# Order of the first DMA requests in a gated-FFN and state-space kernel: two tiles of token block 1 ahead of the first LoRA factors

## The chip, the cores and the metric

The kernel runs on one core of one Trainium2 chip. The metric is the device time of the kernel in microseconds (us). Three runs of the kernel before the change gave 439.82, 440.07 and 442.02 us; their median is 440.07 us.

## The reference

```python
x = L0_attn_u                                   # (2, 1024, 512) float32
xn = _layernorm(x, axis=-1)                     # over the 512 features of a token
s = _L0_attn_ref(xn, ...)                       # S4: a causal convolution of length 512 along the
                                                # features, plus D * xn; its kernel K comes from
                                                # a 64-state system by way of an FFT
g = _silu(_L0_ffn_ref(xn, w1, w3, w2, A1, B1, A3, B3, A2, B2))
x = x + s * g
...
def _lora_linear(x, w, a, b):                   # w, with a LoRA pair a (16 x in), b (out x 16)
    base = jnp.einsum('bsd,od->bso', x, w)
    low = jnp.einsum('bsr,or->bso', jnp.einsum('bsd,rd->bsr', x, a), b)
    return base + low * 2.0
h1 = _lora_linear(x, w1, lora_A1, lora_B1)      # 512 -> 1376
h3 = _lora_linear(x, w3, lora_A3, lora_B3)      # 512 -> 1376
return _lora_linear(silu(h1) * h3, w2, lora_A2, lora_B2)
```

All of it is computed in float32.

## The kernel before

**Tiling.** The 2048 tokens are four blocks of 512 (blocks 0 to 3), each of four tiles of 128 tokens by 512 features (256 KB). The 1376 hidden features are five pairs of 128-wide chunks and a last chunk of 96. The LoRA pairs are not applied to the tokens: TensorE multiplies the small factors (L410), and the product is added to the weights in SBUF, so that one weight matrix is left. The large products are made by a Strassen-like scheme (sums of token blocks and sums of weight blocks, seven products in place of eight, twice nested), whose sums run on VectorE.

**Order of the work.** TensorE, VectorE, ScalarE and GpSimd have a schedule written out by hand: the program's order is the order on each engine, and every engine takes its own instructions strictly in order. The main part is put into a heap of events with places (the function `at`), and run off in order of place. DMAs are issued from two queues, those of SP (`nc.sync`) and ScalarE (`nc.scalar`). ScalarE issues DMAs from the same stream as its compute, so a DMA issue that waits holds up what stands behind it on ScalarE.

**Semaphores of the DMAs.** In the built program the DMAs of both queues take eight semaphores in turn, in program order. A DMA that takes a semaphore for the second time waits at its issue until the DMA that had it before has landed. The first eight DMAs wait for nothing. The ninth waits for the first, the tenth for the second, and so on.

**The start (L1020 to L1074).** These steps are what the change and the prediction touch:

- `load_x(0)` at L1020 (the DMA itself is L236): four tiles of block 0, SP takes tiles 0 and 2, ScalarE takes tiles 1 and 3.
- `load_lora` at L1027: the first factors. The inner factors a1 and a3 (16 x 512, 32 KB each, L399, tile `lo_d`) and the columns 768 to 1375 of the outer factors b1T and b3T (16 x 608, 38 KB each, L400, tile `lo_h`). SP loads a1 and b1T into partitions 0 to 15, ScalarE loads a3 and b3T into partitions 32 to 47.
- The activation at L1028 loads ScalarE's table ahead of its use.
- `load_x(1)` at L1029: four tiles of block 1, all on SP.
- `load_last` (L502): the last chunk of w1T and w3T. `load_pair(0)` (L429): the first weight pair. Blocks 2 and 3 (L236, tile `t_in`), the second pair and two more sets of factors follow on SP.
- `keep_warm` (L1046): 18 dummy products, 36 matmul instructions, that keep TensorE busy until the data comes.
- `lora_last` (L410, banks y) and `pair_products(0, 0)` (L410, banks x and w): the first real products of TensorE. They need the first factors.
- `take_last` (L520): ScalarE takes the two y banks out to SBUF, scaled.
- `norm_stats` (L252, L253), `norm_root` (L286, L57 to L66, L289) and `normalize` (L298 on ScalarE for tiles 0 and 2, L302 on GpSimd for tiles 1 and 3): the layer norm of block 0. VectorE makes the statistics.
- `merge_last` (L528) on GpSimd adds the taken-out products to the last chunk of weights.
- `transpose` (L309): TensorE turns the four tiles of block 0, and ScalarE copies them out (L317). The products of the last chunk follow (L799).
- The same layer norm is made for block 1 (L252 to L289, L298, L302), whose tiles are turned at L329.

On ScalarE the order is therefore: DMA issues, table load, the two L520, the two L298 of block 0, the copies L317. On TensorE it is: L1046, L410, L309, L799.

## Time and profile before

| what | value |
|---|---|
| median of three runs | 440.07 us |
| profiled execution, its own time | 439.75 us |
| its span, first to last instruction | 437.7 us |
| granted TensorE clock, mean | 0.999 |
| busy TensorE / VectorE / GpSimd / ScalarE | 431.7 / 314.3 / 211.4 / 146.8 us |
| moved by DMA in the span | 53.60 MB, mean 122 GB/s |

The profile is of one execution. "Busy" is the time in which an engine had an instruction in work. A row of a timeline gives the start, the duration, the engine, the line, the operation, the tile that is written and those that are read, the count and, in brackets, the idle time ahead of it and what ended it. SPq and ACTq are the issuing of DMAs by SP and ScalarE, PEld is the loading of weights into TensorE.

### The profile page before, as it was taken

The numbers are of one execution on the slowest core, as the hardware profiler recorded it, in microseconds if no ns is written. First come the engines' busy times: TensorE is split into PE (matmuls) and PEld (weight loads), VectorE is DVE, ScalarE is ACT, GpSimd is POOL, SyncE is SP. The second block draws the span as 40 slices with busy tenths as digits, with TensorE's granted clock in tenths as the row PEclk, the third lists the DMA queues.
The fourth block names the chain that finished last, engine by engine and source line by source line (L and its number), as shares of the span: only waits on it lengthen the run. The fifth ranks groups of instructions, "written<-read, shape, count | busy, mean of one in ns | idle before, by whom it ended". The sixth has DMA issues, their size and how long they took to land.

```text
span 437.7 us, 5081 instructions
## 1 busy us (share of the span) xinstructions
PE 431.7 (99%) x1664; PEld 267.7 (61%) x1664; DVE 314.3 (72%) x531; ACT 146.8 (34%) x301; POOL 211.4 (48%) x159
## 2 busy tenths in 40 slices
PE   7999999999999999999999999999999999999996
PEld 7645334344444444444443447888898999989896
DVE  5989997975873687368736786979786885653234
ACT  2897233344344334433443242211101212112221
POOL 1628185799599558945894378400000122222221
PEclk9999999999999999999999999999999999999999
DMA  8931312016105200430054536395901833422211
GB/s 242 368 96 27 130 59 91 0 50 206 35 24 158 84 25 24 148 113 24 25 173 164 168 98 209 114 355 195 361 3 74 303 124 96 145 96 97 77 68 48
DMA packets 35465, 53.60 MB, mean 122 GB/s; under 512 B 4688, under 2 KB 21520, under 8 KB 35312
## 3 DMA queue, kind: packets, MB, share of 16 engines
q1 hardware_dynamic: 31824, 49.55, 33.9%
q10 hardware_dynamic: 3616, 3.74, 2.9%
q8 instruction: 13, 0.21, 0.2%
q14 instruction: 12, 0.10, 0.1%
HBM read 33.88 MB, written 19.40 MB: 122 GB/s over the span
## 4 chain that ended last, share of the span: by engine, by line
PE 88%; DVE 8%; ACT 1%; issue 1%; DMA 1%; POOL 0%; SPq 0%; DVEq 0%; ACTq 0%; POOLq 0%
PE x L799 44%; PE y L799 22%; PE w L799 12%; PE aux L979 2%; PE w L979 2%; PE aux L994 2%; DVE xt L355 2%; DMA s<-in_x_dram 1%; DVE s L485 1%; PE y L410 1%; DVE w L473 1%; PE y L572 1%; PE aux L754 1%; ACT c L259 1%; DVE aux L1379 1%
## 5 line engine op out<-in xcount | busy, mean ns | idle before, releaser
L1382 POOL TENSOR_TENSOR o<-o,xin 128x512 f32<-128x512 f32 (+1 forms) x17 | 23.3, 1369 | 132.5 <-DMA g<-g_dram 68.6
L885 POOL TENSOR_TENSOR s<-c,s 128x512 f32<-128x512 f32 (+1 forms) x44 | 66.0, 1505 | 11.5 <-ACT c L877 7.7
L819 ACT COPY s<-x 128x512 f32<-128x512 f32 (+1 forms) x54 | 31.6, 585 | 82.7 <-PE x L799 77.7
L799 PE MATMUL x<-t_in,s 128*128 128x512 f32 (+1 forms) x148 | 55.4, 500 | 0.0
L823 DVE TENSOR_TENSOR s<-s,y 128x512 f32<-128x512 f32 (+1 forms) x54 | 36.4, 681 | 18.4 <-PE y L799 10.6
L919 POOL TENSOR_TENSOR s<-ua_three,s 128x512 f32<-128x512 f32 x20 | 30.2, 1510 | 21.6 <-DVE s L823 21.6
L799 PEld LDWEIGHTS x<-t_in,s 128*128 128x128 f32 x148 | 26.8, 190 | 22.4 <-issue 12.4
L919 POOL TENSOR_TENSOR ua_three<-ua_three,s 128x512 f32<-128x512 f32 x20 | 31.2, 1560 | 14.0 <-DVE s L823 14.0
L799 PE MATMUL y<-t_in,s 128*128 128x256 f32 (+1 forms) x108 | 35.8, 458 | 0.0
L1404 ACT COPY z<-x 128x256 f32<-128x256 f32 x24 | 8.8, 371 | 70.4 <-PE x L799 70.3
L1379 DVE TENSOR_TENSOR aux<-aux,m 128x384 f32<-128x384 f32 x32 | 18.1, 566 | 15.7 <-PE aux L979 14.1
L919 POOL TENSOR_TENSOR s<-u_three,s 128x512 f32<-128x512 f32 x20 | 28.4, 1423 | 1.8 <-ACT c L877 1.0
L877 ACT ACTIVATE c<-c 128x512 f32<-128x512 f32 x40 | 25.2, 632 | 10.4 <-DVE c L919 10.2
L799 PEld LDWEIGHTS y<-t_in,s 128*128 128x128 f32 x108 | 20.2, 190 | 11.1 <-issue 9.1
L919 POOL TENSOR_TENSOR u_three<-ua_three,u_three 128x512 f32<-128x512 f32 x10 | 15.9, 1589 | 20.5 <-DVE u_three L823 18.2
L842 ACT COPY w<-x 128x512 f32<-128x512 f32 (+1 forms) x37 | 21.1, 571 | 11.8 <-PE x L799 11.7
L799 PE MATMUL x<-t_in,w 128*128 128x512 f32 x40 | 21.0, 606 | 0.0
L799 PE MATMUL x<-xr,w 128*128 128x512 f32 x40 | 20.8, 613 | 0.0
L799 PE MATMUL x<-xt,w 128*128 128x512 f32 x40 | 20.6, 597 | 0.0
L799 PE MATMUL x<-xr,s 128*128 128x512 f32 x40 | 20.5, 614 | 0.0
L799 PE MATMUL x<-xt,s 128*128 128x512 f32 x40 | 20.4, 592 | 0.0
L799 PE MATMUL y<-xt,w 128*128 128x512 f32 x40 | 19.9, 592 | 0.0
(321 smaller groups left out, 911.7 us busy)
## 6 DMA issues: line engine op xcount, KB each, us to landing
g_dram<-s SPq DMA_DIRECT2D x40, 256.0 KB, 2.2
g<-g_dram SPq DMA_DIRECT2D x10, 512.0 KB, 5.8
xin<-in_x_dram SPq DMA_DIRECT2D x16, 256.0 KB, 2.7
out_dram<-o SPq DMA_DIRECT2D x14, 256.0 KB, 2.0
t_in<-g_dram SPq DMA_DIRECT2D x6, 512.0 KB, 4.2
t_in<-in_x_dram SPq DMA_DIRECT2D x8, 256.0 KB, 5.4
w_a<-in_w2T_dram SPq DMA_DIRECT2D x2, 1024.0 KB, 7.1
room<-g_dram SPq DMA_DIRECT2D x4, 512.0 KB, 6.1
```

Source lines behind the costliest of these rows:

```text
L355: nc.vector.tensor_tensor(t[name - 1], one, other, add if name == 2 else sub)
L799: nc.tensor.matmul(ps[:, cols], lhsT=lhsT, rhs=rhs if parts == 1 else rhs[:, cols], start=first and i == 0 and part == 0, stop=i == len(pa ...
L819: nc.scalar.copy(t, self.x)
L823: nc.vector.tensor_tensor(t, t, self.y, add)
L842: nc.scalar.copy(self.w, self.x)
L877: nc.scalar.activation(c, c if src is None else src, AF.Silu)
L885: nc.gpsimd.tensor_tensor(g, act, g, mult)
L919: (nc.vector if o < 20 else nc.gpsimd).tensor_tensor(to, a, b, add)
L979: nc.tensor.matmul(to[:, n * P : (n + 1) * P], lhsT=x_, rhs=by, start=start, stop=True, skip_group_check=True,)
L1379: nc.vector.tensor_tensor(y[:, P:], y[:, P:], m[:, n * P : (n + 3) * P], add)
L1382: (nc.vector if last else nc.gpsimd).tensor_tensor(o, o, self.xin[h][:, cols], add)
L1404: nc.scalar.copy(t, xb)
```

## The change

The first eight DMAs in program order are now the four tiles of block 0, tiles 0 and 1 of block 1, a1 and a3. Then come b1T and b3T, and then tiles 2 and 3 of block 1. Tiles 1 and 3 of block 1 go to ScalarE's queue in place of SP's. ScalarE's table load stands behind all of these. No DMA and no compute instruction is added or taken away, and the order of the compute instructions on each engine stays as it was.

```diff
-    def load_x(b):
+    def load_x(b, some=range(NTT)):
...
-        for tt in range(NTT):
+        for tt in some:
...
-            queue = nc.scalar if b == 0 and tt % 2 else nc.sync
+            queue = nc.scalar if b < 2 and tt % 2 else nc.sync
...
         if d is not None:
             queue.dma_start(out=lora["d"][rows, :], in_=d)
+        if h is None:
+            return
         queue.dma_start(out=lora["h"][rows, : hi - lo], in_=h[:, lo:hi])
...
     factors = (a1, b1T), (a3, b3T)
-    for v, f in enumerate(factors):
-        load_lora((nc.sync, nc.scalar)[v], v, *f, LSPLIT, HID)
+    x_in[1] = load_x(1, (0, 1))
+    for v, (d, h) in enumerate(factors):
+        load_lora((nc.sync, nc.scalar)[v], v, d, None, LSPLIT, HID)
+    for v, (d, h) in enumerate(factors):
+        load_lora((nc.sync, nc.scalar)[v], v, None, h, LSPLIT, HID)
+    x_in[1] += load_x(1, (2, 3))
     nc.scalar.activation(warm, warm, AF.Silu)
-    x_in[1] = load_x(1)
     make_upper_triangular(nc, tri, 1.0, diag=True)
```

## Prediction

> **What bounds the kernel now.** I read the page's engine rows first, then the list of what TensorE (PE) waited for, then the timelines of the first 12 us engine by engine, then the DMA views of that stretch.

> ```profile
> PE 431.7 (99%) x1664; PEld 267.7 (61%) x1664; DVE 314.3 (72%) x531; ACT 146.8 (34%) x301; POOL 211.4 (48%) x159
> ...
> PE w L1046 <- POOL ident masks.py:199: 1.4, 1, 1.4
> PE aux L309 <- ACT s L298: 1.0, 1, 1.0
> ```

> The second and third lines are the whole of PE's waits in 437.7 us. PE waits 1.4 us at the start for the identity, 1.0 us for the first normalized tile of block 0, and from 11.0 us on it waits for nothing that the list shows: its instructions follow one another to 434.1 us. The end is therefore the start of the first transpose (L309, at 10.99 us) plus a fixed 426.7 us. Whatever moves L309 moves the end one for one; what is moved elsewhere is free until it makes PE wait. A little can be absorbed: between 53 and 59 us three matmuls start 0.1 to 0.2 us late, 0.4 us in all, since VectorE (DVE) has only just made their operands.

> So the question is what sets 10.99 us. The timelines of PE, ScalarE (ACT) and DVE from 5 to 12 us (start, duration):

> ```profile
> 5.58 2.50 PE L1046 MATMUL w<-ident 128*128 128x128 f32 x17
> 8.01 1.13 PE L410 MATMUL y<-lo_h,lo_d 16*128 16x96 f32 x16
> ...
> 9.66 0.37 PE L410 MATMUL w<-lo_h,lo_d 16*128 16x256 f32 x1
> 10.99 0.44 PE L309 MATMUL aux<-ident,s 128*128 128x128 f32 x2 [0.96 <-ACT s L298]
> ```
> ```profile
> 9.17 0.87 ACT L520 ACTIVATE c<-y 128x384 f32<-128x384 f32 x2 [5.09 <-PE y L410]
> 10.12 1.52 ACT L298 ACTIVATE s<-s,shift,rs_y 128x512 f32<-128x512 f32 x2
> ```
> ```profile
> 6.40 0.69 DVE L252 BATCH_NORM_STATS2 stats<-s 128x6 f32<-128x512 f32 x1 [0.84 <-DMA s<-in_x_dram]
> 7.13 0.18 DVE L253 BATCH_NORM_AGGREGATE mv<-stats 128x2 f32<-128x6 f32 x1
> ...
> 9.93 0.16 DVE L289 SCALAR_TENSOR_TENSOR shift<-mv,rs_y 128x4 f32<-128x4 f32 x1
> ```

> L309 needs L298, and L298 has two conditions of almost the same age. One is DVE's shift, ready at 9.93 + 0.16 = 10.09 us; the chain of waits goes this way, back to tile 2 of block 0, which landed at 6.38. The other is ACT's own order: the two L520 end at 9.17 + 0.87 = 10.04 us. They wait for PE's L410, which starts at 8.01, and L410 waits for the four factors. Their landings:

> ```profile
> lo_h<-in_b1T_dram SPq DMA_DIRECT2D x1, 38.0 KB, 5.6
> lo_h<-in_b3T_dram ACTq DMA_DIRECT2D x1, 38.0 KB, 5.8
> ```

> Issued at 2.09 and 2.11 us, they land at 7.7 and 7.9. The dummy products would let PE go at 7.92 (the last starts at 7.80, and they start 0.11 apart). The factors therefore come just in time, with no reserve, and ACT's branch trails DVE's by 0.05 us.

> **The change part by part.**

> *Block 0 lands earlier.* Tiles 2 and 3 landed at 6.38 and 6.96 (issued at 1.15, 5.2 and 5.8 us to landing) while the factors were coming in. With tiles 0 and 1 of block 1 behind them in place of the factors, I expect them between 4.9 and 5.3: 1.05 MB at the 370 GB/s of the first row below end at 4.8. DVE then loses its 0.84 us of waiting: the shift is ready at about 9.2. Alone this is worth at most 0.08 us, since the L520 hold ACT until 10.04 even with the factors as early as now. That is the bound on the gain.

> *The factors land later.* 512 KB now go ahead of them. The DMA traffic in three stretches (last two columns: busy share, GB/s):

> ```profile
> 2.00:5.00 3.00, 3.00 (x16) 3.00 (x16) 1.10 (x3) 1.49 (x2) 0.00 (x0) 1.00 1.03 370
> 5.00:7.00 2.00, 2.00 (x13) 2.00 (x13) 1.13 (x3) 0.00 (x0) 0.00 (x0) 1.00 1.04 131
> 7.00:10.00 3.00, 3.00 (x34) 2.46 (x32) 2.59 (x14) 0.83 (x2) 0.00 (x0) 1.00 1.04 343
> ```

> While the factors are under way (5 to 7 us) the engines are as busy as before but move a third; afterwards the rate returns. So the tiles ahead pass at the full rate: 524 kB / 370 GB/s = 1.4 us, and the slow stretch follows, as long as now. The last factor lands at 7.9 + 1.4 = 9.3 us. Two checks on this: b1T and b3T are the ninth and tenth DMA now, so they wait for tiles 0 and 1 of block 0, landed at 3.84 and 4.02, and are issued at 3.9 and 4.0 in place of 2.1, still 2 us before their turn; and the first other tiles of block 1 are issued at about 5.1, behind them, and share the slow stretch as block 1's tile 0 did before (issued at 3.86). Lower bound: no slow stretch at all; 1.57 MB + 0.14 MB at 370 GB/s end at 6.6, landing about 7.0, so PE is not held and the change gives -0.1. Upper bound: the 524 kB pass at 131 GB/s, 4.0 us, so +3.9. I take 1.4, since the rows on both sides of the slow stretch carry tiles of just this kind at 343 and 370.

> *What the late factors hold.* L410 moves from 8.01 to about 9.4, the L520 from 9.17 to 10.57, ACT is free at 11.44 in place of 10.04, L298 starts at 11.45 in place of 10.12, and L309 at 12.3 in place of 10.99: +1.3 us. PE's own order alone (L410 issued until 9.87 + 1.4 = 11.3) would not bind. Behind ACT's L520 also wait the copies L317, behind PE's L410 everything; GpSimd's (POOL) L528 need the L520 too and move with them. DVE's merges (L420 at 15.99, after a wait for PE of 0.2) move with PE. I let 0.2 us be absorbed, half of the late starts found at 53 to 59 us: **+1.1 us**.

> *Block 1's statistics.* DVE reaches them at 9.2 in place of 10.0, and needs tiles 0 to 3 at 9.2, 10.0, 10.8 and 11.6. They land by about 6.5 (0, 1) and 9.6 to 10.4 (2, 3; the total of bytes up to there is unchanged, and tile 3 landed at 10.36). No wait. This branch was not late before: L298 of block 1 ended at 16.59, PE came to L329 at 16.82. Worth nothing.

> *Later loads on SP.* The same eight semaphores, two requests fewer on SP. The first weight pair now waits for the landings of a1, a3, b1T and b3T (about 8.6 to 9.3) and was issued from 8.37 to 9.94 before: no change over 0.3 us. Its pieces landed at 12.5 to 14.7, and DVE takes them from 16.0: 1.3 us of cover, more if PE is late.

> *ACT's table load.* It ran from 2.58 to 3.86. It now stands behind tile 3 of block 1, whose issue waits for tile 3 of block 0 (at the latest 6.96, as now): issue to 7.4, load to 8.7, the small activation to 8.9. The first L520 came at 9.17: hidden by 0.3 us in that worst case, by 1.5 us or more with the later factors.

> [...] The factors go to partitions 0 to 15 and 32 to 47, and the row says 131 GB/s for 2 us. [...] The row shows 2 us, and 3 from the end of block 0's data (4.8) to the last landing (7.9); I follow it.

> **Rivals.**

> *Hidden (439.6 to 440.3).* The slow stretch comes from factors and tiles of both queues in each other's way, and is shorter when the factors come in one after another, or the 512 KB fill time that was lost. The factors land by 8.4, the time changes by -0.1 to +0.4. For it: four factor loads with 48 KB each, issued from 29.3 to 30.6 us with nothing beside them, landed in 1.9 to 2.0 us. Against it: at 5 to 7 us the tiles beside them were slow as well, and tiles are beside them again.

> *The clock falls (443.3).* PE has a hole of 1.4 us at 8 to 9.4 in which it had none, then 1.9 us of 16-row matmuls, then a second hole of 1.0 us. If TensorE's granted clock drops over this, the transposes start at the pace of the beginning: dummy products start 0.213 us apart until 6.4 us, 0.112 after, and that stretch, 5.1 us, cost 23 x 0.101 = 2.3 us. With +1.3 and less absorbed, +3.5. It decides from a hole that the clock does not forgive. Against it: the hole of 1.1 us before L309 cost no clock; the L309 start 0.109 apart.

> [...]

> *The slow stretch grows (442 to 443.6).* The tiles ahead of the factors also come in at the slow rate: up to the upper bound of +3.9.

> *It gains.* Only if L309 moved forward by 2.2 us; the L520 forbid this.

> **How the numbers follow.** 0.5% is 2.2 us, about what a measurement of this kernel can tell from no change. The sum against the profiled execution: 439.75 (span 437.7 and 2.05 around it) + 1.1 = 440.85. The median of the runs lies 0.3 above that execution, which would give 441.2; I say 441.0. Chances: forecast (+0.4 to +2.2) 0.65; hidden 0.19; clock 0.08; slow stretch beyond 2.2 us 0.06; a gain 0.02. Faster 0.02, within 0.65 + 0.19 = 0.84, slower 0.14. The range goes from 439.6 (hidden, -0.1) to 442.9, into the slow cases, and leaves the clock's case and the far end out.

> **What would show it.** Right: DVE's wait before L252 gone and the shift near 9.2; landings of b1T and b3T near 9.3; a wait of PE before L410; L298 of block 0 right behind the L520 at about 11.4; L309 near 12.3; no other PE wait. Wrong: factors landed by 8.0 (hidden), L309 starts 0.21 apart (clock), ACT's L520 behind the table load, or a new wait of DVE for block 1.

## The result and the profile after

The changed kernel takes 443.05 us (median of nine runs, 441.54 to 444.96) against 440.07 us before. The ratio is 1.0063, with a 95% interval of 1.0041 to 1.0085: slower by 0.6%. The profiled execution is the slowest of the nine, 444.96 us, with a span of 442.9 us and a mean granted clock of 0.991.

The engine row and the row of the clock in 40 slices, from the page of the changed kernel, and then the whole list of what TensorE (PE) waited for. Lines of the file have moved: L412 was L410, L522 was L520, L801 was L799, L1051 was L1046.

```profile
PE 434.5 (98%) x1664; PEld 269.6 (61%) x1664; DVE 314.8 (71%) x531; ACT 147.0 (33%) x301; POOL 211.6 (48%) x159
...
PEclk9699999999999999999999999999999999999999
```
```profile
PE y L412 <- DMA lo_h<-in_b1T_dram: 2.6, 1, 2.6
PE w L1051 <- POOL ident masks.py:199: 1.4, 1, 1.4
PE y L801 <- DVE w_a L422: 0.4, 1, 0.4
PE aux L309 <- ACT s L298: 0.4, 1, 0.4
```

The same row of the clock from the page of the kernel before:

```profile
PEclk9999999999999999999999999999999999999999
```

Two things are new. PE waits 2.6 us for the factors, where it waited for none. And the second slice of the clock row has a 6 where every slice had a 9: for a stretch behind the start, TensorE got half its clock (0.50, in the table of stretches below). The landings of b1T and b3T, issued at 4.03 and 4.22 us, come to 9.9 and 10.1:

```profile
lo_h<-in_b1T_dram SPq DMA_DIRECT2D x1, 38.0 KB, 5.9
lo_h<-in_b3T_dram ACTq DMA_DIRECT2D x1, 38.0 KB, 5.9
```

The timelines of PE and ScalarE (ACT), start and duration, show the chain that the prediction followed:

```profile
9.96 1.20 PE L412 MATMUL y<-lo_h,lo_d 16*128 16x96 f32 x15 [2.58 <-DMA lo_h<-in_b1T_dram]
...
12.75 1.97 PE L309 MATMUL aux<-ident,s 128*128 128x128 f32 x8 [0.38 <-ACT s L298]
14.51 1.91 PE L309 MATMUL y<-ident,s 128*128 128x128 f32 x8
...
19.25 1.13 PE L412 MATMUL aux<-lo_h,lo_d 16*128 16x256 f32 x8
```
```profile
11.12 0.87 ACT L522 ACTIVATE c<-y 128x384 f32<-128x384 f32 x2 [3.79 <-PE y L412]
11.88 1.51 ACT L298 ACTIVATE s<-s,shift,rs_y 128x512 f32<-128x512 f32 x2
```

The rows of the kernel before to set beside them:

```profile
10.99 1.09 PE L309 MATMUL aux<-ident,s 128*128 128x128 f32 x8 [0.96 <-ACT s L298]
...
14.82 1.13 PE L410 MATMUL aux<-lo_h,lo_d 16*128 16x256 f32 x8
```

The first eight L309 take 1.97 us where they took 1.09. By start times, from L309 to the L412 on aux is 12.75 to 19.25 = 6.5 us; it was 10.99 to 14.82 = 3.8. Cut where the clock changes, and into stretches of 3.4 us, half of the 6.8 us at half clock, ahead of it (the columns: length, busy time of PE, PEld, DVE, ACT, POOL, granted clock, DMA share, GB/s):

```profile
5.00:8.40 3.40, 2.38 (x21) 2.19 (x20) 3.09 (x12) 1.49 (x2) 0.00 (x0) 1.00 0.94 253
8.40:11.80 3.40, 1.84 (x24) 1.80 (x24) 3.16 (x12) 0.68 (x2) 1.52 (x2) 1.00 0.76 205
11.80:18.60 6.80, 6.42 (x25) 5.12 (x23) 3.41 (x12) 3.94 (x7) 5.07 (x9) 0.50 1.02 350
18.60:22.00 3.40, 3.40 (x20) 2.01 (x20) 1.58 (x3) 2.11 (x4) 0.94 (x2) 0.99 1.06 373
```

PE was busy for 2.4 and 1.8 of 3.4 us, and then had half its clock for 6.8 us, while it was busy nearly throughout.

The span grew by 442.9 - 437.7 = 5.2 us in this execution: 1.8 us until L309 (12.75 against 10.99), 2.7 us at half clock, and 0.8 us later (442.9 - 19.25 = 423.7 behind the L412 on aux, against 422.9). Instruction by instruction, PE runs 4.43 us behind the kernel before at 17 us and 4.45 behind it at 230 us. Then 0.7 us is lost at one place, at 240 us: the merge of w2 (L422) waited for the second half of w2, which took 9.5 us from issue to landing, against 8.5 in the profile before and 8.2 to 8.8 in the profiles of all eleven experiments. The last 0.1 comes at 313 us. No other profile shows the loss at 240 us, so it belongs to this one execution as far as is known.

### The profile page after: what moved, and what is told of

The parts are those of the page before. It is cut to its first block, busy times and chain, and to the rows that moved or that the text cites. A ratio compares the mean times of both kernels' runs of the same rounds, so it can differ in the third digit from the quotient of the medians.

```text
span 442.9 us, 5080 instructions
## 1 busy us (share of the span) xinstructions
PE 434.5 (98%) x1664; PEld 269.6 (61%) x1664; DVE 314.8 (71%) x531; ACT 147.0 (33%) x301; POOL 211.6 (48%) x159
## 4 chain that ended last, share of the span: by engine, by line
PE 83%; DVE 6%; DMA 5%; POOL 3%; issue 1%; ACT 1%; SPq 0%; POOLq 0%; DVEq 0%; ACTq 0%
PE x L801 40%; PE y L801 21%; PE w L801 11%; PE w L981 2%; PE aux L981 2%; DMA w_a<-in_w2T_dram 2%; DMA lo_h<-in_b1T_dram 2%; PE aux L996 2%; DVE xt L355 2%; POOL s L921 1%; PE y L412 1%; POOL s L887 1%; DVE s L487 1%; DMA s<-in_x_dram 1%; PE aux L756 1%
## 5 line engine op out<-in xcount | busy, mean ns | idle before, releaser
L801 PE MATMUL x<-t_in,s 128*128 128x512 f32 (+1 forms) x148 | 55.4, 500 | 0.0
L801 PEld LDWEIGHTS x<-t_in,s 128*128 128x128 f32 x148 | 26.8, 190 | 22.4 <-issue 12.2
L801 PE MATMUL y<-t_in,s 128*128 128x256 f32 (+1 forms) x108 | 35.9, 459 | 0.4 <-DVE w_a L422 0.4
L879 ACT ACTIVATE c<-c 128x512 f32<-128x512 f32 x40 | 25.2, 633 | 11.4 <-DVE c L921 11.2
L801 PEld LDWEIGHTS y<-t_in,s 128*128 128x128 f32 x108 | 20.1, 190 | 11.9 <-issue 8.8
L801 PE MATMUL x<-t_in,w 128*128 128x512 f32 x40 | 21.0, 606 | 0.0
L801 PE MATMUL x<-xr,w 128*128 128x512 f32 x40 | 20.8, 613 | 0.0
L801 PE MATMUL x<-xt,w 128*128 128x512 f32 x40 | 20.6, 597 | 0.0
L801 PE MATMUL x<-xr,s 128*128 128x512 f32 x40 | 20.5, 614 | 0.0
L801 PE MATMUL x<-xt,s 128*128 128x512 f32 x40 | 20.4, 592 | 0.0
L801 PE MATMUL y<-xt,w 128*128 128x512 f32 x40 | 19.9, 592 | 0.0
```

Of the source, the lines that this page charges most:

```text
L801: nc.tensor.matmul(ps[:, cols], lhsT=lhsT, rhs=rhs if parts == 1 else rhs[:, cols], start=first and i == 0 and part == 0, stop=i == len(pa ...
L879: nc.scalar.activation(c, c if src is None else src, AF.Silu)
```

## The experiments

Each run's mean granted clock is on record, and it sorts the runs. Beside the experiments the kernel before ran 81 times. In 69 of these the clock was 0.998 or more and the median 439.80 us; in 12 it was 0.994 or 0.995 and the median 441.1 us. In the changed kernel it was 0.996 or less in nine of nine. I call a run "at full clock" from 0.998 on.

**The order alone and the queues alone.** Order alone: the changed kernel with

```diff
-            queue = nc.scalar if b < 2 and tt % 2 else nc.sync
+            queue = nc.scalar if b == 0 and tt % 2 else nc.sync
```

> The changed kernel with all four tiles of block 1 on SP, so the order alone. Theory (it is the 512 KB ahead of the factors that make them late): a1 and b1T land at 9.5 to 10.2, TensorE waits for them 2 us and more, 442 to 444. Rival (the second queue is what delays them, since both queues carry tiles beside the factors): factors by 8.5, 440 to 440.8.

Measured: 441.81 us, ratio 1.0041 (1.0026 to 1.0056), no run at full clock out of six. The last factor lands at 8.6, between the two expectations: a3 and b3T, no longer behind a tile on ScalarE's queue, land by 7.8. PE waits 1.0 us for the factors and 0.6 us behind their products, and the clock falls in every run.

Queues alone: the kernel before with `b < 2` in place of `b == 0`, and the activation that loads the table behind `load_x(1)`.

> The kernel before with tiles 1 and 3 of block 1 on ScalarE's queue, and the first factors ahead of block 1 as before; the table load stands behind the issue of tile 3. Theory (order, not queues): factors at 7.6 to 8.2, L309 at 10.9 to 11.3, full clock, 439.8 to 440.4. Rival (ScalarE's blocked issue and the table load behind it are what costs): the table load ends after 9.2, the evictions at L520 come later than 9.4, 440.6 to 441.5.

Measured: 440.03 us, ratio 1.0003 (0.9992 to 1.0015), ten of twelve runs at full clock. The queues alone cost nothing; the order costs 0.4%. The two together cost 0.6%, 1.2 us more than the order alone. That tile 1 of block 1 then stands ahead of a3 and b3T on ScalarE's queue fits this, and was not tested by itself.

**A hole in TensorE without any change of DMAs.** The kernel before with

```diff
-        keep_warm(ps, 9, True)
+        keep_warm(ps, 6, True)
```

> The kernel before with 12 dummy products in place of 18: its DMAs are untouched, TensorE has a hole of 1.5 to 2.1 us ahead of L410 at 8.0. Theory (the hole alone sets the clock): if such a hole is enough, L309 starts at 11.0 as before but the clock is halved there, 441.4 to 442.8; if it is not enough, 440.1 and the full clock. Rival (the late factors themselves cost the time, by what waits for them, and the clock falls only with them): 440.1 and the full clock in any case.

Measured: 442.33 us, ratio 1.0058 (1.0038 to 1.0077), no run at full clock out of six. The wait of PE, and three stretches of that kernel:

```profile
PE y L410 <- DMA lo_h<-in_b1T_dram: 1.4, 1, 1.4
```
```profile
4.50:8.00 3.50, 2.13 (x25) 1.97 (x24) 3.24 (x11) 0.00 (x0) 0.00 (x0) 1.00 1.02 279
8.00:14.80 6.80, 6.80 (x34) 5.85 (x32) 6.09 (x25) 4.70 (x8) 3.78 (x6) 0.50 1.06 335
14.80:18.00 3.20, 3.20 (x17) 1.89 (x16) 0.67 (x3) 1.71 (x4) 2.97 (x5) 1.00 1.05 386
```

Here the factors were not late (7.05 and 7.25) and L309 even came earlier, at 10.54, yet the kernel is 2.4 us slower: a hole of 1.4 us ahead of the factors' products makes the clock fall with no change of DMAs, and the rival that let the clock fall only with late factors is out. What the clock follows is not the hole alone; see below.

**Filling the hole.** The changed kernel with 30 dummies (`keep_warm(ps, 15, True)`):

> The changed kernel with 30 dummy products in place of 18, so that TensorE is busy until about 9.9 us. Theory (the late factors leave TensorE idle from 7.2 to 10.0 us, and this hole makes the granted clock fall): the factors still land near 10 us and L412 still starts near 10.0, but the clock stays full, L309 start 0.11 us apart, and L309 to the fifth product group (L412 on aux) takes 3.8 us as before the change, in place of 6.5. The time falls by the 2.7 us that the half clock cost in the profile, to 441.0 to 442.2, still 1 to 2 us over the kernel before. Rival (the clock is indifferent to the hole, or the time is lost elsewhere): the half clock is still there and the time stays at 442.5 to 444.

Measured: 443.67 us, ratio 1.008 (1.0056 to 1.0105). The row of dummies was too long: in the profiled execution the dummies ran until 11 us although the factors were there at 9.1, so they held L412 until 11.19. By the time it decides nothing. By the clock it says something: three of six runs are at full clock, and these took 441.95 to 443.04, the others 444.31 to 445.11.

A second trial has 24 dummies ahead of L412 and 3 behind it:

```diff
-        keep_warm(ps, 9, True)
+        keep_warm(ps, 12, True)
...
     ps_pair = [pair_products(0, 0, numbered("x1", "w1"))]
+    keep_warm(primed[0], 3)
```

> The changed kernel with 24 dummy products ahead of L412 in place of 18, and 3 more between L412 and the first transposes, so that both idle stretches of TensorE are filled and less than in the kernel with 30, where the dummies themselves held L412 until 11.2. Theory (late factors cost up to 2 us, the clock falling behind them 1.2 us or more per window of 3.4 us): the granted clock is 0.998 and more in most runs, and these take 441 to 442; the median falls by 0.8 us and more against the changed kernel's 443.05. Rival (the clock falls whatever is put there, since the 16-row matmuls of L412 alone let it fall): clock 0.996 and less in all runs, 443 to 444.5.

Measured: 441.71 us, ratio 1.0044 (1.0027 to 1.0061). Seven of twelve runs are at full clock, median 441.38; the other five took 442.67 to 443.67. The profiled execution is one of the seven, and the list of PE's waits is down to the identity:

```profile
PE w L1051 <- POOL ident masks.py:199: 1.4, 1, 1.4
```

This splits the loss, with these seven runs standing in for the changed kernel at full clock, which none of its own nine runs shows. At full clock the changed order costs 441.38 - 439.80 = 1.6 us, the late factors; in the profile L309 starts at 12.47, 1.5 us later than before. The remaining 443.05 - 441.38 = 1.7 us of the median is the clock.

**The same filling in the kernel before.** Four dummies between L410 and the transposes (`keep_warm(primed[0], 4)`), nothing else.

> The kernel before with 4 dummy products between L410 and the first transposes, where TensorE is idle for 1.0 us. Theory (that stretch, beside the 16-row matmuls, is what lets the clock fall in some runs of the kernel before: 441.1 us at clock 0.995 in 2 of 17): no run with a clock below 0.997, all runs 439.2 to 440.4, median 439.7 to 440.0. Rival (the clock falls by chance, whatever stands there): one or two runs in ten at 441 still.

Measured: 439.72 us, ratio 0.9997 (0.9988 to 1.0006), twelve of twelve runs at full clock, 439.25 to 440.19. The median hardly moves; the runs at 441 are gone. With 12 falls in 81 runs of the kernel before, none in twelve could still be chance about once in seven times.

**Why the factors are slow.** Groups 1 and 2 of the factors exchange their partitions, in `load_lora` and `lora_factors`, so that a3 and b3T go to 64 to 79 in place of 32 to 47:

```diff
-        rows = slice(32 * group, 32 * group + R)
+        at_ = 32 * (0, 2, 1, 3)[group]
+        rows = slice(at_, at_ + R)
```

In the kernel before:

> The kernel before with the same exchange of partitions. Theory: the stretch from 5 to 7 us carries more than 131 GB/s and the factors land by 7.2 in place of 7.9, but TensorE is held by its dummies until 7.9 and ScalarE by L520, so 439.5 to 440.1. Rival: landings at 7.1 to 7.9 as before, 439.7 to 440.2; the two are told apart by the landings and the rate, not by the time.

In the changed kernel:

> The changed kernel with the factors of group 1 in partitions 64 to 79 in place of 32 to 47 (groups 1 and 2 exchanged). Theory (the slow stretch is due to the 16-row factors, all written into few partitions): if 32 to 47 and 0 to 15 share their way into SBUF, the stretch is shorter, the last factor lands at 8 to 8.8 in place of 9.1 to 10.1, 441.3 to 442.3. Rival (what is slow does not depend on the partitions): landings and time as in the changed kernel, 442.4 to 443.6.

Measured: 439.92 us, ratio 0.9997 (0.9984 to 1.0011), for the kernel before; 440.97 us, ratio 1.0026 (1.001 to 1.0042), for the changed one, with six of twelve runs at full clock, median 440.25. The same two views that the prediction showed of the kernel before, now with the other partitions: landings in us behind an issue at 2.09 and 2.11, and the stretches.

```profile
lo_h<-in_b1T_dram SPq DMA_DIRECT2D x1, 38.0 KB, 4.5
lo_h<-in_b3T_dram ACTq DMA_DIRECT2D x1, 38.0 KB, 4.6
```
```profile
2.00:5.00 3.00, 3.00 (x16) 3.00 (x16) 0.99 (x3) 1.49 (x2) 0.00 (x0) 1.00 1.01 364
5.00:7.00 2.00, 2.00 (x12) 2.00 (x12) 1.93 (x5) 0.00 (x0) 0.00 (x0) 1.00 1.02 277
7.00:10.00 3.00, 3.00 (x35) 2.57 (x33) 2.59 (x14) 0.72 (x2) 0.56 (x1) 1.00 0.92 273
```

From 5 to 7 us the DMA engines carry 277 GB/s in place of 131, and the last factor lands at 6.75 in place of 7.91. The other profiles with these DMAs agree: 298 GB/s and 6.74 with the new partitions; 157, 157 and 191 GB/s and 7.8, 7.7 and 7.2 with the old ones. So the slow stretch goes with where the two sets of 16 rows are written: 131 to 191 GB/s with partitions 0 to 15 and 32 to 47, 277 and 298 with 0 to 15 and 64 to 79. Why, no run shows. In the changed kernel the last factor lands at 8.9, and at 9.3 in the kernel of the next trial, where three kernels with the same first DMAs and the old partitions had 9.1, 9.6 and 10.1. These landings overlap; what shows the gain there is the time, 440.97 against 443.05 us with the same dummies.

**What is left of the change.** The changed kernel with those partitions, 20 dummies ahead and 3 behind:

> The changed kernel with group 1 in partitions 64 to 79, 20 dummy products ahead of the factors' products and 3 behind. Theory (what is left of the change's loss, once the slow stretch is shortened and TensorE is kept busy, is the 512 KB ahead of the factors): factors at 8.5 to 8.9, L309 at 11.4 to 11.7, full clock in most runs, 440.2 to 440.7. Rival (the order itself costs nothing then): 439.6 to 440.0.

Measured: 440.43 us, ratio 1.0023 (1.0007 to 1.0039); eight of twelve runs at full clock, median 440.35. So 0.55 us is left at full clock against 439.80: the order by itself costs, though a third of what it cost with the old partitions and 24 dummies. The profiled execution is one of the four that lost the clock: its dummies ended at 8.1 and PE waited 1.1 us for the factors.

**A version that beats both.** The kernel before with the other partitions, 14 dummies ahead of L410 and 4 behind:

> The kernel before with three edits that the runs so far point to: group 1 of the factors in partitions 64 to 79, 14 dummy products ahead of L410 in place of 18, 4 dummies between L410 and the transposes. Theory (the start of the transposes is set by the factors' landing, by the dummies ahead of L410 and by VectorE's shift, and the clock by TensorE's idle time): factors land near 6.8, the shift is ready near 9.3, L309 starts at 10.1 to 10.4 in place of 11.0, the clock stays full in most runs, 439.0 to 439.5. Rival (the shorter row of dummies opens a hole that lets the clock fall more often than the bridge saves): clock 0.996 in several runs, median 439.9 to 441.

Measured: 439.32 us, ratio 0.9987 (0.9976 to 0.9998), twelve of twelve runs at full clock, 438.72 to 439.86. The gain is 0.1%, and the interval only just leaves out no change. Its PE and ACT:

```profile
6.79 1.19 PE L412 MATMUL y<-lo_h,lo_d 16*128 16x96 f32 x16
...
8.80 1.16 PE L1048 MATMUL w<-ident 128*128 128x128 f32 x8
...
10.29 1.09 PE L309 MATMUL aux<-ident,s 128*128 128x128 f32 x8 [0.33 <-ACT s L298]
```
```profile
7.95 0.87 ACT L522 ACTIVATE c<-y 128x384 f32<-128x384 f32 x2 [3.87 <-PE y L412]
9.42 1.52 ACT L298 ACTIVATE s<-s,shift,rs_y 128x512 f32<-128x512 f32 x2 [0.60 <-DVE shift L289]
```

The factors' products start at 6.8, ACT is free 0.6 us before VectorE's shift, and L309 moves from 10.99 to 10.29.

The same without the exchange of partitions:

> The kernel before with 14 dummy products ahead of L410 and 4 behind, the factors' partitions as they were. Theory: the factors land at 7.1 to 7.9 as before, so the shorter row of dummies frees L410 by 0.3 us at most and leaves a hole in some runs; 439.4 to 440.0, between the kernel with the bridge alone (439.72) and the one with the other partitions. Rival (the partitions add nothing to the time): the same time as that one, within 0.1 us.

Measured: 439.93 us, ratio 1.001 (0.9997 to 1.0024), seven of twelve runs at full clock, median 439.74; PE waited 1.5 us for factors that landed at 7.7. Without the partitions the shorter row of dummies opens the hole again, so the shorter row needs the partitions, and the rival falls. The partitions and the four dummies behind L410 without the shorter row were not run together.

**What the clock follows.** In the profile of this last kernel PE waited 1.5 us and the clock stayed full. In the profile with the other partitions, 20 dummies ahead and 3 behind, it fell although PE was busy for 3.19 us of the 3.41 ahead of the fall:

```profile
4.23:7.64 3.41, 1.91 (x18) 1.75 (x16) 2.93 (x8) 0.00 (x0) 0.00 (x0) 1.00 1.07 249
7.64:11.05 3.41, 3.41 (x36) 3.07 (x37) 3.03 (x14) 2.18 (x4) 1.24 (x2) 1.00 1.06 309
```
```profile
8.92:12.33 3.41, 3.19 (x33) 2.86 (x34) 3.21 (x10) 2.03 (x4) 2.86 (x5) 1.00 0.98 245
12.33:15.74 3.41, 3.41 (x17) 3.27 (x16) 2.16 (x11) 2.33 (x5) 1.70 (x4) 0.50 1.04 360
```

| profile | window | other products | 16 rows | idle | clock behind it |
|---|---|---|---|---|---|
| changed kernel | 8.43 to 11.84 | 0.00 | 1.88 | 1.53 | half |
| changed, 30 dummies | 10.94 to 14.35 | 0.69 | 1.96 | 0.76 | half |
| queues alone | 7.53 to 10.95 | 1.05 | 1.96 | 0.41 | half |
| changed, other partitions, 20 + 3 | 8.92 to 12.33 | 1.07 | 2.13 | 0.22 | half |
| order alone | 9.17 to 12.59 | 1.09 | 1.69 | 0.64 | half |
| before, 12 dummies | 4.55 to 7.97 | 1.27 | 0.78 | 1.37 | half |
| before, 14 + 4 | 7.65 to 11.06 | 1.34 | 2.07 | 0.00 | full |
| before, other partitions, 14 + 4 | 5.80 to 9.21 | 1.47 | 1.94 | 0.00 | full |
| before, other partitions | 6.71 to 10.12 | 1.48 | 1.93 | 0.00 | full |
| before | 6.48 to 9.90 | 1.60 | 1.82 | 0.00 | full |
| changed, other partitions | 6.46 to 9.87 | 1.61 | 1.15 | 0.65 | full |

The clock fell behind each window with at most 1.27 us of other products and behind none with 1.34 or more until the last product. The idle time does not sort the rows. The 16-row products therefore seem to count for little (0.78 to 2.13 us of them stand in the windows ahead of a fall, 1.15 to 2.07 in the others), and the stretch of the factors' products is as much a part of the fall as the waits around it. This was read off afterwards, and the limit is not sharp: behind the last product the clock fell after windows with up to 1.4 us. To get the full clock back took more: a window with 2.51 us in the changed kernel did not do it, one with 3.06 in the kernel with the queues alone did.

## Why the prediction was right or wrong

The likeliest case, 441.0 us, did not come; the time lies at the rival "the clock falls" (443.3), 0.15 us above the end of the range. That the rival's number fits so well is in part luck: it put 1.3 us on the late factors, less what is absorbed, and 2.3 on the clock, and they cost 1.6 and 1.7. By steps:

- **What bounds the kernel** held. The start of L309 and PE's clock behind it explain the change; from the L412 on aux to the end the kernels here take 423 us each (422.9 before, 423.1 in the kernels with the order alone and the queues alone, 423.7 in the changed kernel's profile).
- **Block 0 lands earlier** held. Tiles 2 and 3 landed at 5.22 and 5.43 (said: 4.9 to 5.3), the shift was ready at 9.30 (9.2). As said, it gained nothing, since ACT stood at L522.
- **The factors land later** was right in kind and too small. Said: 9.3. Landed: 10.1 in the profile, 9.1 and 9.6 in two kernels with the same first DMAs. Two sizes were off, in opposite directions. The landing at 7.9 in the one profile of the kernel before was the latest of five with the factors ahead of block 1 (7.1, 7.2, 7.7, 7.8, 7.9), so the starting point was too late. And the tiles ahead cost more than 1.4 us, 1.9 from middle to middle, since they did not pass at the full rate: tiles 0 and 1 of block 1, said to land by 6.5, landed at 8.99 and 9.34, caught in the slow stretch with the factors behind them.
- **What the late factors hold** held link by link. L412 to L309 took 2.8 us (said: 2.9).
- **0.2 us absorbed later** failed: from 17 to 230 us nothing was absorbed, and 0.8 us was added behind that in the profiled execution.
- **Later loads on SP** failed in their times. SP stood until 9.0 for tile 0 of block 1, so the first pair was issued from 10.0 in place of 8.37 (said: no change over 0.3). The cover held: GpSimd waited 1.0 us for the last chunk, PE for none of these.
- **The table load** ran from 5.84 to 7.12, hidden as said.
- **The step that decided** was the rival's weight. The clock's fall was priced about right (2.3 us; 2.7 in the profile, 1.7 in the median) and given a chance of 0.08, "Against it: the hole of 1.1 us before L309 cost no clock". That was true of one execution (the hole is 0.96 us there). In 12 of 81 executions the kernel before lost its clock too, with no hole but that one in its profile, so the kernel stood at the edge, and with 1.0 us (order alone) to 2.6 us more of waiting every run was over it. The forecast itself put the clock at nothing; it cost 1.7 us, about half of the loss.

**The clock's fall in time.** Half clock lasted 6.8 us in the changed kernel's profile and in the one with 12 dummies, and 3.4 us in the one with the order alone. In the six windows ahead of a fall PE was busy for 1.88 to 3.19 of 3.41 us: none of them was idle throughout.

**Open.** That 16-row products count for little is read from profiles that were made for other ends; a kernel with the waits and without these products, or the reverse, was not run. Where the windows lie differs from profile to profile (the full clock came between 4.2 and 7.5 us). That this is why some executions of one kernel lose the clock and others not is the author's guess; no run sets it.

## What to carry to other kernels

Where TensorE has no other waits, read what feeds its first real product, and price a late feed twice: once for the shift, once for the clock that the wait may cost (1.6 and 1.7 us here). A hole that one profile shows to be harmless is no proof (0.96 us in the kernel before, where 12 of 81 runs lost the clock); the granted clocks of many runs say more. In the kernel before, four dummy products across the hole left no run out of twelve below full clock; in the changed kernel dummies brought seven of twelve runs back. Small transfers into few partitions deserve a look at where they land: moving one of two sets by 32 partitions cost nothing and brought the last of them in 0.4 to 1.2 us earlier in the kernel before.

## What the runs showed of the hardware that was not expected

The full clock came between 4.2 and 7.5 us after the span's start in thirteen profiles, with TensorE busy from 1.4 us on in all of them (in the kernel before, dummy products start 0.213 us apart ahead of it and 0.112 behind it), so the same 18 dummies ended at 7.4 us in the changed kernel's profile and at 8.6 in that of the queues alone. That is why a fixed count both held the factors' products back in some executions and left a hole in others.

TensorE's order was not quite strict. In the changed kernel's profile, where the second set of factors landed last, a product of L412 on x (first set) started at 10.93 us, ahead of the last one on y (second set) at 11.01, which the program has before it.
